# Two-layer graph attention: input groups of the other batch entries share the eight-buffer ring of the first one

## The chip, the cores and the metric

The kernel runs on one core of one Trainium2 chip. The time is device time in microseconds (us) of one execution, and the figure compared is the median of several runs.

## The reference, cut to what matters

The input x has 8 batch entries of 2048 rows of 256 numbers; adj is a 2048 x 2048 matrix of 0 and 1 shared by all entries. Two layers follow each other, each with a residual and a layer norm.

```python
# layer 0: 8 heads of 32 columns; prior is adj itself
x_proj = einsum('bnd,hdf->bhnf', x, W)
e = leaky_relu(e_src[..., :, None] + e_dst[..., None, :], 0.2) + softplus(beta_tilde) * log(prior + 1e-6)
attn = softmax(where(adj > 0, e, -max), axis=-1)
h = einsum('bhij,bhjf->bhif', attn, x_proj)          # heads joined to 256 columns
x = layernorm(x + h @ W_out.T)
# layer 1: one head, scores are dot products
h1, h2, h3 = x @ W1, x @ W2, x @ W3
e = where(adj > 0, leaky_relu(h1 @ h2^T, 0.2), -1e12)
x = layernorm(x + relu(softmax(e, axis=-1) @ h3))
```

## The kernel before, in words

Layer 0 of an entry is done by a `Gat`, layer 1 by a `Dot`. A `Gat` works in 4 passes (`hp`, two heads each) of 16 steps (`jt`, 128 source rows each), 64 steps in all. In a step VectorE (DVE) writes two tiles `s`, 128 x 2048 fp32, one for each head (L391: the larger of the query factor `c` and the source factor `re`, times the column of M, `mt`), and TensorE (PE) multiplies them into `val` and `den` (L424). Entry 0 goes first and alone; from then on, the Gat of entry b is interleaved with the Dot of entry b-1.

In its first pass entry 0 also makes M from adj. `make_m` (L187 to L192) loads a column block of adj and makes a tile `m` with DVE and ScalarE (ACT); `make_mt` turns it with PE (L201), copies it with ACT (L202) and stores it to `mt_d` (L203). All later passes load `mt` from there (L208). The query factors `c` are loaded from `c_d` at each pass (L328) into two buffers; those of entry 1 are asked for after entry 0's last step by `load_ahead`.

Beside entry 0's 64 steps run the projections of the seven other entries, in the generator `others`. It works in 28 groups of 512 rows: `load_x` fetches a group of x (L173), `transpose_x` turns it on PE (L181) and copies it with ACT (L182), and `Gat.row` projects 128 rows at a time (L283), copies them (L285, L287) and hands them, four rows together, to the store of `v_d` (L668). After the last group of an entry, `factors` makes the entry's exponentials (L293 to L301, with DVE, POOL and ACT) and stores them to `re_d` (L671). After every second step `others` is advanced by three or four rows. Group n+1 is turned (`turn`) after the second row of group n.

The buffers of the ring are the tag "s" of the pool `wide`: eight buffers of 128 x 2048 fp32. They hold the `s` tiles, the `m` tiles of the first pass, the first x tiles (`first_x`), `xt0` until entry 0's own rows are projected, and, from the end of entry 0's third pass, its second tile of heads, `ht`. The x groups of the other entries use the tag "pen" with one buffer, which is not used for anything else until layer 1 begins.

The order of PE's work is the order of the program (`manual_schedule`). DVE, ACT, POOL and, through entry 0, SyncE's DMA queue (SP) are ordered by the planner of the framework when the kernel is built. From entry 1 on SP's order is that of the program too. `evict` and `finish` move a pass's results out: copies (L439), reciprocals (L445 to L449), the broadcast load `rb` (L461) and the product (L467).

Of the kernel before, what the change touches and what calls it, by code (L numbers as in the profile page):

```python
# [9 lines left out]
F32 = mybir.dt.float32  # L10
# [8 lines left out]
P = 128  # L19
# [8 lines left out]
def kernel(  # L28
# [27 lines left out]
    B, N, D = x.shape  # L56
# [8 lines left out]
    IG = BK // P  # L65
# [8 lines left out]
    wide = ctx.enter_context(tc.tile_pool(name="wide", bufs=2))  # L74
# [8 lines left out]
    def ring_tile(name, shape=(P, N)):  # L83


        return wide.tile(list(shape), F32, tag="s", name=name, bufs=8)
# [82 lines left out]

    def load_x(b, g):  # L170

        xg = wide.tile([P, IG, D], F32, tag="pen", name="xg", bufs=1)
        nc.sync.dma_start(xg, x[b].rearrange("(t p) d -> p t d", p=P)[:, ts(g, IG), :])  # L173
        return xg

    def transpose_x(xg, dst):

        for kc in range(KC):
            t = mm_tile("tr")
            for k in range(IG):  # L180
                nc.tensor.transpose(t[:, ts(k, P)], xg[:, k, ts(kc, P)], ident)  # L181
            nc.scalar.copy(dst[kc], t)  # L182
# [456 lines left out]
    def others():  # L639

        order = gats[2:-2] + gats[1:2] + gats[-2:]
        groups = [(gat, g) for gat in order for g in range(NB)]
        xgs, xts = [], []

        def load(n):
            if n < len(groups):
                xgs.append(load_x(groups[n][0].b, groups[n][1]))

        def turn(n):
            if n < len(groups):  # L650
                xt = chunk.tile([P, KC, BK], F32, tag="ht", name="xt", bufs=4)
                xts.append([xt[:, kc, :] for kc in range(KC)])
                transpose_x(xgs[n], xts[n])
                load(n + 1)

        load(0)
        yield
        turn(0)
        for n, (gat, g) in enumerate(groups):
            if g == 0:  # L660
                gat.begin()
            v = chunk.tile([P, NP, IG, HP * DH], F32, tag="v", name="v", bufs=2)
            for k in range(IG):
                gat.row(g * IG + k, xts[n], v[:, :, k, :])
                if k == 1:
                    turn(n + 1)
                if k == IG - 1:
                    nc.sync.dma_start(v_d[gat.b].rearrange("h p t f -> p h t f")[:, :, ts(g, IG), :], v)  # L668
                if g == NB - 1 and k == IG - 1:
                    gat.factors()  # L670
                    nc.sync.dma_start(re_d[gat.b], gat.re)  # L671
                if g == 0 and k == IG - 1 and n > 0:
                    groups[n - 1][0].queries()
                yield
        order[-1].queries()
        yield

    projections, weights = others(), later_weights()
    next(projections)
    count = (B - 1) * NT  # L680
# [87 lines left out]
```

## Time and profile before

| | us |
|---|---|
| median of 3 runs (lowest, highest) | 4265.29 (4264.81, 4266.23) |
| the profiled execution, its own time | 4269.6 |
| its span, first to last instruction | 4267.8 |
| PE busy | 4169.3 (98%) |
| DVE busy | 3617.9 (85%) |
| ACT busy | 1606.5 (38%) |
| mean granted clock of TensorE | 0.995 |

The profile is one execution. A busy PE is not a PE at its peak, since matmuls are pipelined and their ends are modelled. A wait names what came last by the trace; a DMA's wait for its buffer is listed as SP's own wait. Lines such as L173 are line numbers of the kernel before.

### The profile page before, as it was taken

The page shows a single profiled execution, that of the slowest core. Times are in us where ns is not written, and L with a number is a line of the kernel's source. Part 1 is how long each engine was busy: PE and PEld are TensorE (multiplying, and loading weights), DVE is VectorE, ACT ScalarE, POOL GpSimd, SP SyncE. Part 2 cuts the span into 40 slices and gives each one's busy share as a digit, 9 for nine tenths or more (in the row PEclk, how much of TensorE's full clock was granted, in tenths as well). Part 3 has the DMA queues.
Part 4 walks back from the last instruction along what each step waited for, and adds up shares of the span by engine and source line. Part 5 has one row for each costly group of instructions (what it writes and reads, how often), then busy time and mean ns, then how long its engine had stood idle before and what let it go on. Part 6 is the DMA issues. An engine that isn't in the chain of part 4 may idle for free.

```text
span 4267.8 us, 59104 instructions
## 1 busy us (share of the span) xinstructions
PE 4169.3 (98%) x24928; PEld 2234.3 (52%) x24928; DVE 3617.9 (85%) x2432; ACT 1606.5 (38%) x3007; POOL 10.3 (0%) x14
## 2 busy tenths in 40 slices
PE   7999999999999999999999999999999999999999
PEld 4444355555555555555555555555455555555766
DVE  6888779998899979999799988999799997998222
ACT  6522133332333333332433333333333323343554
POOL 0000000000000000000000000000000000000000
PEclk9999999999999999999999999999999999999999
DMA  7988756656455565556555474555555565553211
GB/s 240 312 281 322 243 205 225 235 203 238 175 203 201 192 212 181 193 191 226 187 203 194 161 250 166 204 194 204 204 186 189 182 233 180 203 187 136 78 48 40
DMA packets 268458, 843.52 MB, mean 198 GB/s; under 512 B 33184, under 2 KB 166304, under 8 KB 194464
## 3 DMA queue, kind: packets, MB, share of 16 engines
q1 hardware_dynamic: 232352, 806.17, 53.7%
q10 hardware_dynamic: 35840, 33.57, 2.3%
q8 instruction: 195, 3.19, 0.3%
q14 instruction: 71, 0.58, 0.0%
HBM read 763.76 MB, written 75.37 MB: 197 GB/s over the span
## 4 chain that ended last, share of the span: by engine, by line
PE 57%; DVE 26%; issue 8%; DMA 4%; ACT 4%; SPq 0%; DVEq 0%; POOL 0%; ACTq 0%; POOLq 0%
DVE s L391 16%; PE acc L607 13%; PE e L564 12%; PE val L424 12%; PE den L424 8%; DVE d L404 5%; PE pt L590 3%; DMA mt<-mt_d 2%; PE h3p L532 2%; PE proj L283 2%; PE h1p L553 2%; DVE p L569 2%; PE y L493 1%; ACT d L409 1%; DMA adj_r<-in_adj_dram 1%
## 5 line engine op out<-in xcount | busy, mean ns | idle before, releaser
L391 DVE SCALAR_TENSOR_TENSOR s<-c,re,mt 128x2048 f32<-128x2048 f32 x1024 | 2358.4, 2341 | 180.9 <-DMA mt<-mt_d 58.0
L424 PE MATMUL val<-s,v 128*32 128x512 f32 x8192 | 980.3, 598 | 24.1 <-DVE s L391 24.1
L564 PE MATMUL e<-x1t,h 128*128 128x512 f32 x2048 | 964.7, 595 | 6.1 <-ACT pts L592 5.1
L607 PE MATMUL acc<-h,pts 128*128 128x256 f32 x4096 | 907.5, 380 | 0.0
L607 PEld LDWEIGHTS acc<-h,pts 128*128 128x128 f32 x4096 | 779.5, 190 | 157.4 <-issue 57.4
L424 PE MATMUL den<-s,re 128*32 128x512 f32 x5600 | 686.2, 594 | 0.0
L404 DVE SCALAR_TENSOR_TENSOR d<-s,re,d 128x2048 f32<-128x2048 f32 x282 | 654.2, 2342 | 0.0
L424 PEld LDWEIGHTS val<-s,v 128*32 128x32 f32 x8192 | 252.6, 110 | 601.5 <-issue 528.5
L569 DVE CUSTOM_DVE_ANT_0 p<-p,pen 128x2048 f32<-128x2048 f32 x128 | 292.6, 2286 | 256.2 <-ACT p L566 256.1
L564 PEld LDWEIGHTS e<-x1t,h 128*128 128x128 f32 x2048 | 351.2, 190 | 271.7 <-issue 249.8
L566 ACT ACTIVATE p<-e 128x512 f32<-128x512 f32 x512 | 306.1, 598 | 392.9 <-PE e L564 387.5
L572 ACT ACTIVATE p<-p,neg 128x2048 f32<-128x2048 f32 x128 | 256.5, 2004 | 496.8 <-DVE neg L569 496.8
L424 PEld LDWEIGHTS den<-s,re 128*32 128x32 f32 x5600 | 190.3, 110 | 419.4 <-issue 419.0
L590 PEld LDWEIGHTS pt<-ident,p 128*128 128x128 f32 x2048 | 245.5, 141 | 301.1 <-issue 235.8
L592 ACT COPY pts<-pt 128x512 f32<-128x512 f32 x512 | 297.5, 586 | 200.3 <-PE pt L590 193.9
L590 PE MATMUL pt<-ident,p 128*128 128x128 f32 x2048 | 310.2, 276 | 15.7 <-ACT p L572 8.3
L230 ACT ACTIVATE f<-mv,eps_ln 128x1 f32<-128x1 f32 x128 | 37.9, 296 | 432.7 <-DVE mv L228 431.7
L612 ACT ACTIVATE z<-acc,rec 128x256 f32<-128x256 f32 x128 | 60.1, 470 | 288.5 <-issue 127.5
L283 PE MATMUL proj<-wp,xt 128*128 128x272 f32 (+1 forms) x512 | 130.6, 400 | 3.6 <-ACT xt L182 1.8
L532 PE MATMUL h3p<-w3s,x1t 128*128 128x256 f32 x512 | 122.7, 383 | 6.4 <-ACT x1t L527 4.7
L493 PE MATMUL y<-wot,ht 128*128 128x256 f32 x512 | 119.0, 385 | 3.5 <-ACT x1t L527 2.1
L285 ACT COPY v<-proj 128x256 f32<-128x256 f32 x128 | 47.2, 374 | 198.0 <-PE proj L283 153.5
(88 smaller groups left out, 1896.4 us busy)
## 6 DMA issues: line engine op xcount, KB each, us to landing
mt<-mt_d SPq DMA_DIRECT2D x496, 1024.0 KB
c<-c_d SPq DMA_DIRECT2D x64, 1024.0 KB
pen<-pen_d SPq DMA_DIRECT2D x112, 512.0 KB
xg<-in_x_dram SPq DMA_DIRECT2D x60, 512.0 KB
adj_t<-in_adj_dram SPq DMA_DIRECT2D x16, 1024.0 KB
mt_d<-mt SPq DMA_DIRECT2D x16, 1024.0 KB
rb<-rec_d SPq DMA_DIRECT2D x128, 128.0 KB
x_d<-ht ACTq DMA_DIRECT2D x64, 256.0 KB
```

What stands on the lines that cost most here:

```text
L283: nc.tensor.matmul(t[:, 0:cols], xt[kc][:, ts(it % IG, P)], wp[:, kc, 0:cols], start=(kc == 0), stop=(kc == KC - 1))
L391: nc.vector.scalar_tensor_tensor(sa, self.cs[a], self.re[:, 0, jt, h:h + 1], mt, ALU.max, ALU.mult)
L404: nc.vector.scalar_tensor_tensor(d, sa, e[:, jt - 1, h:h + 1], d, ALU.mult, ALU.add)
L424: nc.tensor.matmul(dst[ts(q, DH), ts(c, BK)], weights[q % 2], s[q % 2][:, ds(q // 2 * HALF + c * BK, BK)], start=start, stop=stop)
L532: nc.tensor.matmul(t[:, ts(i, D)], x1t[:, kc, ts(2 * (j - lag) + i, P)], w3s[:, kc, :], start=(kc == 0), stop=(kc == KC - 1))
L564: nc.tensor.matmul(t, self.h1[:, kc, ts(it % IG, P)], self.x1t[:, kc, ts(c, BK)], start=(kc == 0), stop=(kc == KC - 1))
L566: nc.scalar.activation(p[:, ts(c, BK)], t, AF.Prelu, alpha=ALPHA)
L569: nc.vector.tensor_tensor_reduce(p, p, pen, -1.0, FMAX, ALU.add, ALU.min, neg)
L572: nc.scalar.activation(p, p, AF.Exp, bias=neg, scale=-1.0, accum_out=den)
L590: nc.tensor.transpose(t[:, ts(k, P)], p[:, ts(g * IG + k, P)], ident)
L592: nc.scalar.copy(pt, t)
L607: nc.tensor.matmul(acc, pts[g][:, ts(k, P)], self.h3[:, j, :], start=(j == 0), stop=(j == NT - 1))
```

## The change

The tile of `load_x` is taken from the ring instead of the one "pen" buffer: a ring tile of 128 x 8 x 256 fp32, of which the first half is filled. `others` asks for the first two groups before it starts, and, once it has turned group n, for group n+2 instead of n+1. Nothing that is computed changes, and the number of loads and their size stay.

```diff
     def load_x(b, g):
-        xg = wide.tile([P, IG, D], F32, tag="pen", name="xg", bufs=1)
+        xg = ring_tile("xg", (P, 2 * IG, D))[:, 0:IG, :]
         nc.sync.dma_start(xg, x[b].rearrange("(t p) d -> p t d", p=P)[:, ts(g, IG), :])
         return xg
...
                 transpose_x(xgs[n], xts[n])
-                load(n + 1)
+                load(n + 2)
 
         load(0)
+        load(1)
         yield
         turn(0)
```

## The prediction

> **What bounds the kernel now.** I read the page first, then a table of busy time by window, then the waits of entry 0, then the timelines of DVE and PE. The page says whose kernel this is:
>
> ```profile
> span 4267.8 us, 59104 instructions
> ...
> PE 4169.3 (98%) x24928; PEld 2234.3 (52%) x24928; DVE 3617.9 (85%) x2432; ACT 1606.5 (38%) x3007; POOL 10.3 (0%) x14
> ```
>
> PE is idle for only 98.5 us in all. The changed loads, L173, run from 9.4 to 446.7 us, so only that stretch and its hand-over to entry 1 can move. The table by window splits it (busy us in the window; PE is the first number, DVE the third):
>
> ```profile
> 0.00:60.00 60.00, 38.35 (x201) 26.43 (x205) 31.58 (x33) 34.55 (x52) 1.07 (x7) 0.89 0.71 214
> 60.00:200.00 140.00, 124.28 (x895) 66.82 (x891) 114.94 (x61) 95.87 (x154) 1.17 (x1) 0.96 0.90 297
> 200.00:445.00 245.00, 243.60 (x1849) 115.64 (x1842) 209.38 (x109) 63.39 (x211) 7.68 (x5) 1.00 0.84 300
> 445.00:500.00 55.00, 49.78 (x385) 20.30 (x384) 42.53 (x24) 10.57 (x32) 0.37 (x1) 1.00 0.72 248
> ```
>
> Pass 0 (to about 192 us, the one that also builds M) leaves PE 15.7 us idle out of 140. Passes 1 to 3 leave it 1.4 us out of 245: nothing can be won there. The hand-over leaves 5.2 of 55.
>
> What did x cost so far? PE's only wait for an x group, in its timeline, and SP's waits between 60 and 200 us (total, times, longest):
>
> ```profile
> 69.97 1.06 PE L181 MATMUL tr<-ident,xg 128*128 128x128 f32 x8 [2.52 <-DMA xg<-in_x_dram]
> ```
> ```profile
> SPq L203 <- ACT mt L202: 36.0, 12, 4.7
> SPq L668 <- ACT both L287: 24.2, 6, 5.5
> SPq L173 <- PE tr L181: 20.4, 8, 5.7
> ```
>
> The load waits on SP for the transposes of the group before it, since there is one buffer, but PE had to wait for the data once, 2.52 us. SP itself stands there for 20.4 us, and for another 36.2 us between 200 and 450; what is queued behind it are loads of adj_t and mt, which DVE seldom waited for.
>
> What the ring does now, in DVE's timeline:
>
> ```profile
> 260.23 9.14 DVE L391 SCALAR_TENSOR_TENSOR s<-c,re,mt 128x2048 f32<-128x2048 f32 x4 [2.54 <-PE den L424]
> ...
> 441.27 9.14 DVE L391 SCALAR_TENSOR_TENSOR s<-c,re,mt 128x2048 f32<-128x2048 f32 x4 [0.93 <-PE den L424]
> 453.02 2.35 DVE L391 SCALAR_TENSOR_TENSOR s<-c,re,mt 128x2048 f32<-128x2048 f32 x1 [2.60 <-PE den L424]
> 461.71 9.25 DVE L391 SCALAR_TENSOR_TENSOR s<-c,re,mt 128x2048 f32<-128x2048 f32 x4 [6.34 <-DMA c<-c_d]
> ```
>
> These stops are DVE finding the ring full: it starts again when PE has finished a step. Setting the starts of s in DVE's timeline beside those of val in PE's, DVE has up to 8 s tiles started beyond the last finished step in passes 1 and 2, up to 7 in pass 3 (one buffer holds `ht`). So the ring is used to its last buffer as DVE's lead.
>
> **What the Trainium skill says.** "Perfetto Trace Analysis", section "Optimization Strategy": a repeated gap on the engine that should be saturated can mean that there is no room for the next tile. The trace agrees for DVE's stops above; PE has no such gap yet. The same page, "Tensor Engine Instruction", says that the queue of DVE keeps strict order: an s tile that waits for a buffer holds up the DVE work behind it. In the trace nothing on DVE starts inside those stops. "DMA Instruction — HWDGE (DVE, Sync)" says that a DMA's semaphore wait lies ahead of its profiled window: L173's 0.38 us hide the waits listed above.
>
> **The change, part by part.** The bytes and the 28 loads remain; each still takes 0.38 us of SP's issue and 0.5 MB.
>
> *Removed: the one buffer's wait.* The 2.52 us at 67.4 go. The mtp transposes that follow at 72.39 need an m whose last DVE instruction ends at 68.33 + 2.29 = 70.62, so 1.8 of them survive on the chain: **-2 us** (0 to -2.5). In the rest of pass 0, PE waits on DVE and ACT, not on x. A freed SP could let adj_t and mt_d move sooner; bounded by PE's idle time I give this 0, with -10 as an end (15.7 less the waits for s and mt copies that stay).
>
> *Moved: load(1).* It goes from 64.70 to just behind load(0) at 9.41, past adj_t (15.18), w3s (16.07) and the store of c_d (25.95) on SP. The issue at 9.41 lasted 5.73 us; doubled, adj_t would be 6 us late, its m step on ACT is at 28.79 and PE first wants it at 41: **0**, covered by the adj_t that is already there; up to +3 if that cover is gone.
>
> *Added: two x tiles and more in the ring.* I assume that buffers of a tag are handed out in program order (the trace has no ring write that overtakes another). Then x tiles from PE's position to two groups beyond DVE's position are alive: two, and a third when DVE has passed a turn that PE hasn't reached. Turns come every 11.7 us or more (L181's starts), a step of PE is 3.45 us of products plus rows, 5.9 on average. Of 8 buffers 5 to 6 are left for s in passes 1 and 2, and 4 to 5 in pass 3.
>
> Pass 0: live at once are 2 m, the two s of the step on PE, the two being written, and 2 or 3 x: 8 or 9. When it is 9, the second s waits for PE's products (3.64 us) instead of following the first (2.35): 1.3 us. Seven turns fall in this pass: at most 9 us; where PE was late anyway it costs nothing. No row shows it. I take **+3** (0 to +9).
>
> Passes 1 to 3: with 4 buffers DVE writes step n+2 only once n is done. A pair takes 4.7 us, two steps with their rows 11.7: PE is still served, with 2 us to spare instead of the 4 to 15 now. What eats 2 us: each of six `factors` on DVE (0.37 + 0.37 + 0.28 and waits for POOL and ACT: up to 6.61 us in this trace), scale (1.22), and the c loads at two pass changes (DVE was stopped for 6.94 us at 277.71). The smallest lead now is 1.2 us, at pass 2, step 5. Who waits is PE. If every factors stop showed, six times 3 us; if none, 0. I take **+4** (0 to +18).
>
> Hand-over: this can be followed tile by tile. Pass 3 has 7 buffers. Now, step 10 ends on PE at 441.22, step 11 at 444.65, step 12 at 452.96, and the last pair's first tile starts at 448.1, its second at 453.02. With groups 27 and 28 of x in the ring until 446.7 and 458, the four starts are two buffers behind: the first tile of the last pair must wait for step 12, 453.0 instead of 448.1, the second follows at 455.4. The c load behind it cannot start before that tile has read the old c:
>
> ```profile
> 445.80 4.62 DVE s L391 x2
> 450.44 11.08 DMA c<-c_d
> 461.52 0.03 issue
> ```
>
> These are lines of the chain of waits: 450.44 becomes 455.4, the restart at 461.71 becomes 466.6. PE's lead at entry 1 falls now from 6.5 us to below zero by step 4 (it waits 1.2 us at 488.15), so the whole shift arrives: **+5** (+2, the shift of the second tile alone, to +7). After 500 us PE is busy 3713.29 of 3768 us and gives nothing back.
>
> **Sum.** -2 + 0 + 3 + 4 + 5 = +10 us. The profiled execution took 4269.6 us (span 4267.8 and 1.8 around it), 4.3 above the median of 4265.29; on the median the forecast is 4275.3, slower by 0.23%. What a measurement tells from no change is about 0.2%, 8.5 us.
>
> **The rivals.** *The lead was more than enough* (not slower; 0.33): PE never starves at 4 to 6 buffers, because a pair is written in 4.7 us and consumed in 5.9. For it: PE is busy 99.4% from 200 to 445. Against: the leads of 1 to 2 us at the pass changes. It decides as long as DVE's leads stay above zero at those places; then -2, and 0 to +5 of the hand-over: 4265, within 0.2%.
>
> *SP was the brake in pass 0* (faster; 0.12): its 20.4 us of standing for transposes delay adj_t and mt_d, and two thirds of PE's 15.7 us come back: -10, 4255. Against: DVE waited for adj_t only once after 60 us, 3.8 us.
>
> *The ring chokes* (slower still; 0.15): an x load whose buffer is released late on PE stands in SP's queue with mt and c behind it, or the planner puts DVE and ACT in another order beyond entry 0. Nothing in the trace prices it; the nearest are the bounds above, +9, +18 and +7 less 2: 4297.
>
> *That the loads still don't lead* would be the case if x(n+2) got its buffer only from group n's own transposes; PE needs x only 11.7 us later and a load lands within some 5 us (64.70 + 5.13), so the forecast would not move.
>
> **How the numbers follow.** Forecast 0.40 for +8.5 to +20, choke 0.15, enough lead 0.33, SP 0.12. Slower is 0.55, same 0.33, faster 0.12. The range leaves out the deep end of the SP case and the upper half of the choke: 4257 to 4294. The forecast's own is 4273.8 to 4285.
>
> **What would show it.** Right: no PE wait for xg near 67 us; DVE's waits for PE den in entry 0 grow from 11.0 us to 40 or more; PE gains waits for s between 200 and 445, busy falling below 99%; the c load ahead of entry 1 starts some 5 us later after the last step than now. Wrong: PE still at 99.4% there and the hand-over unmoved (enough lead), or step 0 of pass 1 earlier than 185 us (SP), or mt and c waits of DVE above 15 us in passes 1 to 3 (choke).

## The result, and the profile after

The changed kernel takes 4276.61 us (median of 9 runs, 4274.13 to 4280.17) beside 4266.41 us for the kernel before (9 runs, 4264.75 to 4271.80): a ratio of 1.0024, 95% interval 1.0015 to 1.0033, slower by some 10 us. The forecast was 4275.3. The number is close, but by luck: of the four terms of its sum that are not zero three were off, and their errors cancelled. What follows takes it apart.

The head of the page of the changed kernel, and its table of busy time by window (as before: PE is the first number, DVE the third):

```profile
span 4275.5 us, 59130 instructions
...
PE 4170.8 (98%) x24928; PEld 2232.3 (52%) x24928; DVE 3618.7 (85%) x2432; ACT 1606.3 (38%) x3007; POOL 10.3 (0%) x14
```
```profile
0.00:60.00 60.00, 37.72 (x197) 26.35 (x197) 31.57 (x33) 33.98 (x51) 1.07 (x7) 0.90 0.78 235
60.00:200.00 140.00, 125.66 (x927) 66.58 (x929) 117.58 (x62) 96.01 (x155) 1.18 (x1) 0.98 0.92 304
200.00:445.00 245.00, 235.10 (x1722) 110.33 (x1720) 191.93 (x101) 61.86 (x204) 7.68 (x5) 0.99 0.81 276
445.00:500.00 55.00, 55.00 (x432) 23.20 (x428) 49.38 (x26) 12.28 (x39) 0.36 (x1) 1.00 0.73 263
```

The busy totals are those of before; the loss is idle time in the third window, where PE is busy 235.10 us instead of 243.60. PE's waits there are these two lines (total, times, longest); before, only the second one existed:

```profile
PE val L424 <- DVE s L391: 8.5, 7, 4.7
PE tr L181 <- ACT xt L182: 1.4, 2, 0.7
```

To place the loss I took from PE's timeline the start of the first `val` matmul of every step (0 to 63 are entry 0's, 16 a pass; 64 and on are entry 1's) and formed intervals, in us:

| | start of 16 | start of 17 | 17-31 | 31-38 | 38-47 | 47-51 | 51-63 | 63-70 |
|---|---|---|---|---|---|---|---|---|
| before | 192.59 | 200.00 | 82.67 | 41.69 | 47.83 | 22.68 | 70.68 | 37.23 |
| changed | 190.13 | 196.36 | 82.23 | **54.87** | 47.84 | **25.77** | 68.74 | 35.93 |

Pass 0 is won (-3.6 us by step 17), the change from pass 1 to 2 loses 13.2, that from 2 to 3 loses 3.1, and the hand-over loses nothing (-1.3). At step 70 the sum is +9.0; the spans differ by 7.7.

**How 13 us are lost.** DVE's timeline of the changed kernel at the change of pass (start, duration, and in brackets the idle time before it with what ended it):

```profile
267.89 6.88 DVE L391 SCALAR_TENSOR_TENSOR s<-c,re,mt 128x2048 f32<-128x2048 f32 x3 [1.19 <-PE den L424]
280.42 2.35 DVE L391 SCALAR_TENSOR_TENSOR s<-c,re,mt 128x2048 f32<-128x2048 f32 x1 [5.65 <-issue]
285.91 2.35 DVE L391 SCALAR_TENSOR_TENSOR s<-c,re,mt 128x2048 f32<-128x2048 f32 x1 [3.13 <-DMA c<-c_d]
...
304.91 1.22 DVE L467 TENSOR_TENSOR ht<-ht,rb 128x1024 f32<-128x1024 f32 x1
...
314.89 1.23 DVE L467 TENSOR_TENSOR ht<-ht,rb 128x1024 f32<-128x1024 f32 x1 [4.24 <-DMA rb<-rec_d]
319.28 11.40 DVE L391 SCALAR_TENSOR_TENSOR s<-c,re,mt 128x2048 f32<-128x2048 f32 x5 [3.16 <-DMA mt<-mt_d]
```

Before, DVE stopped at the same places:

```profile
277.71 2.35 DVE L391 SCALAR_TENSOR_TENSOR s<-c,re,mt 128x2048 f32<-128x2048 f32 x1 [6.94 <-PE tr L181]
...
304.19 1.22 DVE L467 TENSOR_TENSOR ht<-ht,rb 128x1024 f32<-128x1024 f32 x1 [2.15 <-DMA rb<-rec_d]
308.82 1.23 DVE L467 TENSOR_TENSOR ht<-ht,rb 128x1024 f32<-128x1024 f32 x1 [3.40 <-DMA rb<-rec_d]
311.15 9.14 DVE L391 SCALAR_TENSOR_TENSOR s<-c,re,mt 128x2048 f32<-128x2048 f32 x4 [1.11 <-DMA mt<-mt_d]
```

The first stop is for c. The views name no c load at 280.42 and 277.71, but by the trace's landing times the c load that DVE waits for there landed at 280.34 in the changed kernel and at 277.63 in the one before. Before, DVE stopped with a lead of 13 us; now pair 31 (the two s tiles of step 31) is ready 3.8 us before PE wants it, and the two c stops of 5.65 and 3.13 us use that up. Steps 31 to 36 take 34.76 us instead of 30.86: 3.9 of the 13.2 us.

The second stop lies between the pairs 36 and 37, for rb and mt. From the end of pair 36 to the start of pair 37, products included, it is no longer than before, 8.6 us instead of 9.1; but pair 36 is now ready only 2.7 us before PE starts step 36, instead of 11.5. A part of this stop is built into both kernels: at odd steps the tile `mt` has the tag "d", and the two buffers of "d" are those that rb takes as well. So the mt of step 37 can be loaded only when the first product (L467) has read its rb. Before, that product ended at 304.19 + 1.22 = 305.41, and the load was issued at 305.44. In the changed kernel it ended at 304.91 + 1.22 = 306.13, but the load was issued at 312.22. SP's timeline shows what kept it, and what kept c:

```profile
275.53 0.37 SPq L669 DMA_DIRECT2D v_d<-v  x1
275.99 0.46 SPq L315 DMA_DIRECT2D c_d<-est  x1
276.54 0.95 SPq L328 DMA_DIRECT2D c<-c_d  x1
```
```profile
305.02 0.78 SPq L461 DMA_DIRECT2D rb<-rec_d  x2
310.23 0.38 SPq L669 DMA_DIRECT2D v_d<-v  x1
310.66 1.46 SPq L461 DMA_DIRECT2D rb<-rec_d  x2
312.22 4.74 SPq L208 DMA_DIRECT2D mt<-mt_d  x3
```

The second c load was free to go when DVE ended pair 31 at 267.89 + 6.88 = 274.77; it stands behind two stores of projections until 276.54. The last two of the four loads of the second rb stand from 305.80 to 310.66 behind a store of v_d that waits for ACT's copy of PE's rows, and mt stands behind rb. PE then runs dry at step 37:

```profile
321.69 1.91 PE L424 MATMUL val<-s,v 128*32 128x512 f32 x2 [4.70 <-DVE s L391]
323.95 2.78 PE L424 MATMUL val<-s,v 128*32 128x512 f32 x11 [0.35 <-DVE s L391]
325.68 1.06 PE L424 MATMUL den<-s,re 128*32 128x512 f32 x1
326.51 1.07 PE L424 MATMUL val<-s,v 128*32 128x512 f32 x3
326.53 3.18 PE L424 MATMUL den<-s,re 128*32 128x512 f32 x15
```

It waits 5.05 us and then works slowly. The window of that stretch (0.61 is the granted share of the TensorE clock, behind the five engines' busy times):

```profile
322.00:330.00 8.00, 7.65 (x34) 1.58 (x33) 8.00 (x4) 0.00 (x0) 0.00 (x0) 0.61 0.85 290
```

The trace's clock record has half speed for 6.83 us from 321.46, which by estimate (half of 6.83) loses another 3.4 us of work; in the kernel before no such record lies between 201 and 518 us. So this one stop cost some 5.05 + 3.4 = 8.5 of the 9.3 us that steps 36 to 38 took longer. The Trainium skill, "TensorE: Matmul & The Clock Gate", section "What's actually happening", states that the array drops to half its clock after an idle window of about 3.4 us and returns after a busy one; the stop of 4.70 us here agrees, but shorter ones halved the clock too (2.26 and 1.22 us in e5_after_c below).

### The profile page after: what moved, and what is told of

The parts are those of the page before. It is cut to its first block, busy times and chain, and to the rows that moved or that the text cites. A ratio compares the mean times of both kernels' runs of the same rounds, so it can differ in the third digit from the quotient of the medians.

```text
span 4275.5 us, 59130 instructions
## 1 busy us (share of the span) xinstructions
PE 4170.8 (98%) x24928; PEld 2232.3 (52%) x24928; DVE 3618.7 (85%) x2432; ACT 1606.3 (38%) x3007; POOL 10.3 (0%) x14
## 4 chain that ended last, share of the span: by engine, by line
PE 58%; DVE 25%; issue 7%; DMA 6%; ACT 3%; SPq 1%; DVEq 0%; ACTq 0%; POOL 0%
DVE s L391 16%; PE acc L607 14%; PE e L564 13%; PE val L424 12%; PE den L424 8%; DVE d L404 5%; PE pt L590 4%; DMA mt<-mt_d 3%; PE h3p L532 2%; PE h1p L553 2%; PE proj L283 2%; DVE p L569 1%; PE y L493 1%; ACT d L409 1%; DMA c<-c_d 1%
```

## The experiments

Theory A: x costs what it takes from the ring. DVE's lead shrinks and runs out where DVE is stopped, at the change of pass. Theory B: the new order of the queues, or the deeper loads, cost by themselves. Theory C: the short lead costs everywhere.

**e1_own_pair: the two groups ahead, but in other space.** `h3` of layer 1 is unused during entry 0.

```diff
+    x_space = whole.tile([P, 2, IG, D], F32, tag="h3", name="x_space")
     def load_x(b, g):
-        xg = ring_tile("xg", (P, 2 * IG, D))[:, 0:IG, :]
+        xg = x_space[:, g % 2]
```

> The x groups are asked for two ahead as in the change, but lie in two halves of the space of h3, which nothing uses until entry 1; the ring is as before. Theory A (the ring's buffers are what costs: DVE's lead shrinks and runs out where the c loads of a new pass come): the gain of the early load stays and the loss goes, 2 to 4 us faster than before, some 4262 to 4264, no PE wait above 1 us at the changes of pass, DVE started up to 8 tiles ahead again. Theory B (the order of SP's queue and of DVE, which the planner makes anew, or the depth of the loads is what costs): still 5 to 10 us slower than before.

Measured: 4263.21 us, ratio to before 0.9992 (0.9983 to 1.0000). The deeper load is no loss and keeps the gain of pass 0; steps 31 to 38 take 42.10 us again and PE's busy time from 200 to 445 us is 243.60, the figure of before. Theory B's depth falls. DVE's order from pass 1 on is that of before here, so this run does not test its other half, the planner's new order on DVE.

**e2_ring_one: in the ring, one group ahead.**

```diff
-                load(n + 2)
+                load(n + 1)
         load(0)
-        load(1)
```

> The x groups lie in the ring, but only one is asked for ahead, as before the change. Theory A: one ring buffer less is taken than with two ahead, so about half the loss: 2 to 6 us slower than before, and the PE wait for x near 67 us is there again, since the load follows the transposes of the group before it. Theory B: as slow as the change, 8 to 12 us, or no slower than before if the depth is what costs.

Measured: 4271.57 us, 1.0013 (1.0006 to 1.0019): half the loss. Counting loads against transposes in the traces, 2.0 and 1.9 x tiles are alive on average in passes 1 and 2 here, and 2.9 and 2.8 in the changed kernel. The most s tiles that DVE has started from PE's current step on are 5 or 6 here, 5 in the changed kernel, 6 to 8 before. Steps 31 to 38 take 51.87 us, with a stop of 2.54 us and half speed at step 37; steps 47 to 51 are nearly whole (22.91). The miss: PE did not wait for x near 67 us, since a ring buffer comes free without the group before being turned.

**e3_hold: the kernel before, two ring buffers taken away.** They are taken by a one-column memset and given back after the last `factors`.

```diff
+    held = [ring_tile("held") for _ in range(2)]
+    for t in held:
+        nc.gpsimd.memset(t[:, 0:1], 0.0)
...
+        for t in held:
+            nc.gpsimd.tensor_copy(t[:, 0:1], order[-1].re[:, 0, 0, 0:1])
         order[-1].queries()
```

> The kernel before with its x groups as they were; two buffers of the ring are taken by a one-column memset at the start of entry 0's steps and given back after the last projection. Theory A: the loss comes with nothing else changed, 6 to 12 us slower than before, PE waits for s after the changes of pass 1 to 2 and 2 to 3, about as in the change. Theory B: within 2 us of before.

Measured: 4285.30 us, 1.0045 (1.0032 to 1.0057). More than expected, because step 0 starts 5.2 us later (46.12 against 40.88; not pursued) and the buffers stay taken at the hand-over. Steps 31 to 38 take 51.00 us, +9.3, with x loaded exactly as before; PE's timeline has the same stop:

```profile
326.13 1.92 PE L424 MATMUL val<-s,v 128*32 128x512 f32 x2 [6.02 <-DVE s L391]
```

Steps 47 to 51 are unharmed (22.68), against what theory A expected: six s buffers are enough there, five are not while c is late. Steps 63 to 70 take 42.51, +5.3. So missing buffers make most of the loss without any x load in the ring. Both products stand ahead of pair 37 in DVE's order here, as before (in the changed kernel the first stands ahead of pair 36), so the loss at step 37 does not need the planner's new place for them either.

**e4_pass0: the ring for the first seven groups only.**

```diff
+    RINGED = 7
     def load_x(b, g, n):
+        if n < RINGED:
             xg = ring_tile("xg", (P, 2 * IG, D))[:, 0:IG, :]
+        else:
+            xg = wide.tile([P, IG, D], F32, tag="pen", name="xg", bufs=1)
...
-                load(n + 2)
+                if n + 2 < RINGED:
+                    load(n + 2)
+                elif n + 1 >= RINGED:
+                    load(n + 1)
```

> The first seven x groups, those of pass 0, lie in the ring and are asked for two ahead; from the eighth on the single buffer and one ahead, as before. Theory A: pass 0 starts pass 1 some 2 to 4 us earlier as in the change, and the loss of the changes of pass 1 to 2 and 2 to 3 goes: 2 to 4 us faster than before. Theory B: the planner's new order costs again, 3 us slower or more.

Measured: 4260.28 us, 0.9987 (0.9979 to 0.9995). Step 17 starts at 193.96 instead of 200.00, and the rest is as before (31 to 38: 41.68). In pass 0 DVE never has more than two s tiles ahead in any of these kernels, so the ring has room to lend there.

**e5_after_c: the changed kernel, c loaded early.** c of passes 1 and 3 goes to the space of `h3`; each pass's c is asked for at step 8 of the pass before.

```diff
+                if self.b == 0 and jt == 8 and hp + 1 < NP:
+                    self.cs_next = [self.query_rows((hp + 1) * HP + a, c_space[:, a] if hp % 2 == 0 else None)
+                                    for a in range(HP)]
...
-                        self.cs = [self.query_rows(hp * HP + a) for a in range(HP)]
+                        self.cs = self.cs_next or [self.query_rows(hp * HP + a) for a in range(HP)]
```

> The changed kernel, with entry 0's c rows of passes 1 and 3 in the space of h3 and each pass's c asked for at step 8 of the pass before; x in the ring, two ahead, as in the change. Theory A (a short lead costs only where DVE is stopped for a pass's c loads): the 13 us that PE loses between steps 32 and 38 (pass 1 to 2) and the 3 us at steps 48 to 50 go for the most part; 10 to 14 us faster than the change, 4263 to 4267. Theory C (the short lead costs everywhere, at every factors and every load of mt): it stays within 4 us of the change, 4272 to 4277.

Measured: 4261.10 us, 0.9983 (0.9977 to 0.9990): the loss in the sum is gone though 3.0 and 2.9 x tiles still sit in the ring in passes 1 and 2. Steps 47 to 51 take 22.68, steps 31 to 36 take 30.9 again, and 31 to 38 take 47.70: 6.0 us remain, a PE stop of 2.3 us and half the clock for 3.41, where DVE waits 6.78 us for mt. The first product ended at 301.23 there, and mt was issued at 307.54, behind a store of v_d. Theory C falls; A is incomplete, since c is not the only late load.

**e6_before_c: the same on the kernel before.**

> The kernel before, with the same early c loads. Theory A: with eight buffers the lead of 7 to 15 us covers a c load in passes 1 to 3, so nothing is won there; at most 2 to 4 us at the hand-over to entry 1, whose c buffers are then free a pass earlier: 4262 to 4267. Theory C: no gain either, 4266.

Measured: 4269.51 us, 1.0007 (0.9999 to 1.0016). A miss. Pass 1 starts earlier (step 17 at 193.04), but DVE, which no longer stops for c, reaches the products early and waits 9.1 us for rb, and behind them 7.9 us for mt. The products have the same place in DVE's order as before, ahead of pair 37. From the end of pair 36 to the start of pair 37, the two products included, DVE needs 19.4 us with its lead at 12.8, and steps 31 to 38 take 51.44 with eight buffers. A long lead doesn't help behind an instruction that waits for what PE's own results of the last pass are made into, as rb is. Why the two waits grew to more than before was not isolated.

**e7_after_stores: the changed kernel, the stores of v_d, re_d and c_d on ACT's queue.**

```diff
-    nc.sync.dma_start(v_d[...], v)
+    nc.scalar.dma_start(v_d[...], v)
```
(likewise for `re_d` and `c_d`)

> The changed kernel, with the stores of v_d, re_d and c_d of the projections issued from ACT's queue instead of SP's, so that a load of c, rb or mt isn't queued behind a store that waits for PE. Theory A with SP's order as the second half of the stall (the c loads at 272.5 and 276.5 us and the mt load at 312.2 us were queued behind such stores): some 4 to 8 us of the loss come back, 4269 to 4273. If SP's order plays no part: within 2 us of the change; if the stores hold up ACT, slower than the change.

Measured: 4274.58 us, 1.0019 (1.0010 to 1.0028). Inconclusive in the sum: steps 31 to 38 fall from 54.87 to 46.08, so the stores on SP do hold up those loads (DVE's stop ahead of pair 37 falls from 8.6 to 1.5 us), but step 16 starts 5.6 us later and steps 47 to 51 take 29.11. Why pass 0 suffers was not followed up.

**e8_pass0_c: e4 with e5's early c.**

> The version with the first seven x groups in the ring and the rest in the single buffer, with the early c loads as well. Theory A: the pass-0 gain (6 us measured) and what the hand-over gives: 4257 to 4261. Theory C: as without the early c, 4260.

Measured: 4264.09 us, 0.9993 (0.9985 to 1.0001). Step 17 starts at 190.28, the earliest of all, and steps 31 to 38 lose it again (50.69), as in e6: waits of 10.5 us for rb and 8.3 us for mt.

**e9_after_c_stores: e5, and the stores on ACT's queue after pass 0.**

```diff
-                    nc.sync.dma_start(v_d[...], v)
+                    (nc.scalar if n >= 7 else nc.sync).dma_start(v_d[...], v)
```
(likewise for `re_d` and `c_d`)

> The changed kernel with the early c loads, and with the projections' stores (v_d, re_d, c_d) on ACT's queue from the eighth x group on, so only after pass 0. Theory A with SP's order as its second half: what the early c left over, 6.0 us between steps 31 and 38, came from an mt load queued on SP behind rb loads and stores; it goes, steps 31 to 51 take within 2 us of the 112.2 us of the kernel before although the ring still holds three x tiles: 4255 to 4261. If the short lead alone causes the rest: 4260 to 4264, with the stall near step 37 still there.

Measured: 4256.24 us, 0.9974 (0.9963 to 0.9984), the lowest time of all, faster than both kernels. Steps 31 to 38 take 41.68 and 47 to 51 22.76, with 3.1 and 2.9 x tiles alive in passes 1 and 2. PE's waits and busy time from 200 to 445 us, the two views that showed the loss:

```profile
PE tr L181 <- ACT xt L182: 1.4, 2, 0.7
PE tr L181 <- ACT both L288: 0.2, 1, 0.2
PE proj L284 <- ACT both L288: 0.2, 1, 0.2
```
```profile
200.00:445.00 245.00, 243.19 (x1838) 116.86 (x1839) 206.46 (x108) 64.79 (x216) 7.68 (x5) 1.00 0.85 299
```

**e10_before_stores: the control, the same stores on the kernel before.**

> The kernel before, with the same stores on ACT's queue after pass 0: the control. With eight buffers PE is saturated in passes 1 to 3, so SP's order costs nothing there: within 3 us of before. If the stores on SP cost by themselves, 4 us faster or more; if they hold up ACT's copies, slower.

Measured: 4269.34 us, 1.0008 (1.0000 to 1.0016), no gain: with eight buffers the order on SP costs nothing in passes 1 to 3 (31 to 38: 41.68).

**What they settle.** At the second stop a short sum accounts for the traces. PE's products of a step take 3.45 us, and DVE needs 2.35 us for the first tile of pair 37, so PE should wait by what DVE's stop exceeds the lead and 3.45 - 2.35 = 1.1 us more. All in us:

| | lead: pair 36 ready before step 36 | DVE's stop, pair 36 to 37 | stop - lead - 1.1 | PE's first wait in step 37 |
|---|---|---|---|---|
| before | 11.5 | 9.1 | -3.5 | none |
| changed | 2.7 | 8.6 | 4.8 | 4.70 |
| e2, ring, one ahead | 2.7 | 6.5 | 2.7 | 2.54 |
| e3, two buffers held | 3.8 | 11.1 | 6.2 | 6.02 |
| e5, changed, early c | 4.4 | 7.9 | 2.4 | 2.26 |
| e6, before, early c | 12.8 | 19.4 | 5.4 | 5.30 |
| e7, changed, stores on ACT | 2.7 | 1.5 | -2.3 | none |
| e8, ring in pass 0 alone, early c | 14.0 | 21.1 | 5.9 | 5.80 |
| e9, changed, early c, stores on ACT | 5.0 | 2.5 | -3.5 | none |

PE has no first wait in e1, e4 and e10 either, with leads of 11.4 to 13.6 us and stops of 8.1 to 11.2. So it takes a stop that is longer than the lead that is left. The change shortened the lead; the stop was there before, and was covered. With the short ring the stops have to be short as well: c asked for early takes the loss out of steps 31 to 36 and 47 to 51 (e5), and the stores off SP shorten the stop at step 37 (e7, e9). A full ring covers it (before, e1, e4, e10), but not when it grows to 19 us and more (e6, e8).

## Why the prediction was right or wrong

- **x tiles alive, right.** "Two, and a third", leaving 5 to 6 buffers in passes 1 and 2: the trace has 2.9 and 2.8 alive on average there. Counted as the prediction counts it, beyond the last finished step, DVE's lead falls from at most 8, 8 and 7 tiles in passes 1, 2 and 3 to 6 in each; "4 to 5" for pass 3 was too low. They were asked for earlier than two groups' time: 30 to 47 us before their transposes from step 16 on, against 11 mostly.
- **The x wait, -2: right**, if a little small. PE no longer waits for x at 67 us, and step 2 starts at 72.44 instead of 75.31. Moving load(1), 0: step 0 is 0.9 us later.
- **Pass 0, +3: wrong.** The sum of this pass was to be +1 and is -2.5 at step 16. The step that failed is the count of nine live buffers: DVE is never more than two s tiles ahead here, before or after: it makes the m tiles as well and waits for mt (10.4 us before, 4.9 now, between 60 and 190 us), and a full ring stops it once in the changed kernel, for 0.9 us. In e3, two held buffers lengthen steps 1 to 16 by 0.7 us (134.1 against 133.4). Another 1.2 us come by step 17, where the half-speed record is 3.41 us long (at 191.75) instead of 6.83 (at 194.04). That part is luck: PE's waits at step 16 did not get shorter (3.34 and 1.22 us, before 3.07 and 1.22).
- **Passes 1 to 3, +4: the mechanism right, the size wrong.** Measured from step 17 to 63: -0.4 + 13.2 + 0.0 + 3.1 - 1.9 = +13.9, inside the bound of 18 but for another reason. (The -1.9 is mostly a wait of PE for ACT, 1.72 us before step 62, that the changed kernel does not have.) `factors` and `scale`, which the bound was made of, cost nothing; the loss is at the two changes of pass that the text named. Mis-sized was what the stop for rb and mt takes from a shorter lead. The text had the place, "the smallest lead now is 1.2 us, at pass 2, step 5", which is step 37, but named only `factors`, `scale` and the c loads as what uses the lead up, and did not subtract the missing buffers from those 1.2 us: DVE stands for 9.1 us there in the kernel before already. Left out was also the clock, which adds 3.4 us to the stop of 5.05. I had dismissed SP's standing because DVE seldom waited for it; with the short ring it counts, as e7 and e9 show.
- **Hand-over, +5: wrong.** Measured -1.3. The lead did shrink as worked out: pair 63 is ready 5.98 us before PE instead of 10.19, and the first c load goes 8.2 us before step 63 instead of 15.1. But I left the c load its 11.08 us, and it took less. The line of the chain of waits in the changed kernel:

```profile
467.60 5.18 DMA c<-c_d
```

  Before, an x load (446.67), an mt load and a store of v_d were issued in the four microseconds ahead of the c load at 450.44; now the last x load is at 427.18. From the end of pair 63 to the end of pair 64 DVE needs 7.9 us instead of 11.1. That the emptier queue is the cause is an inference; no run isolates it. Where buffers are still missing at the hand-over (e3) the 5 us do appear (+5.3).
- **The rivals.** Enough lead is refuted by PE's 235.10 us. SP as the brake of pass 0 was half right about pass 0 (-3.6 by step 17, 1.2 of it the clock's) and wrong in the sign of the whole. The choke was one step too far, but its queue, loads standing on SP behind something that waits for PE, is what kept the second stop at 8.6 us, where e7 has 1.5; only it was stores, not x loads, that they stood behind.
- **Signs announced.** PE below 99% from 200 to 445 us: yes, 96%. DVE's waits for PE den at 40 us or more: no, 24.8, since much of the lost lead shows as waits for c, mt and rb. The c load of entry 1 later: yes, by 6.9 us against step 63, but it landed 3.0 us before that step, against 4.0 before. Of the signs of being wrong, that of the choke did show: DVE's waits for mt and c from 200 to 445 us are 17.5 us, with the stop of 5.65, where 15 was the mark; before they were 9.2, with that of 6.94.

The total of +10 thus came from -2 + 3 + 4 + 5 where the runs have about -3.6 (pass 0 with the x wait), +13.9 and -1.3: two parts came out lower and one higher, and that they cancelled is luck.

## What to carry to other kernels

A buffer lent from a producer's ring costs nothing while the producer is bound elsewhere (pass 0), and is paid for at the places where the producer is stopped for longer than the lead that is left; look for those stops and compare each with that lead, not the average rates. Before shortening a lead, list the loads that are asked for only when their buffer comes free, the buffers that two kinds of tile share (here mt and rb), and what stands ahead of the loads in their queue. With c early and the stores on another queue, three tiles fewer in the ring cost nothing and the kernel became 0.26% faster than the one before. Unused space of a later stage (here `h3`) was the better lender (e1).

## What the runs showed of the hardware

A stop of PE cost more than its length here, since half speed followed in the clock record. How long it lasted, 3.41 or 6.83 us, did not follow from the stop's length alone:

| kernel and step | PE's waits for s, us | half speed after, us |
|---|---|---|
| before, 16 | 3.07 and 1.22 | 6.83 |
| changed, 16 | 3.34 and 1.22 | 3.41 |
| changed, 37 | 4.70 and 0.35 | 6.83 |
| e2, 37 | 2.54 and 1.22 | 6.83 |
| e5, 37 | 2.26 and 1.22 | 3.41 |

Half of these stretches, 1.7 or 3.4 us, is the estimate of the work that each lost. The c load of one row to 128 partitions, always the same bytes, took 5.18 us from issue to landing at 467.60 and 9.27 us at 276.54 in the changed kernel, and 11.08 us at 450.44 in the one before.
